# Value products move into a rotation of three PSUM banks with the turns, and the weight mixing is spread differently over a feed-forward block

## The chip, the cores and the metric

The kernel runs on one core of a Trainium2 chip. The metric is the device time of one execution in microseconds (us); for the kernel before it was 3378.83 us, the median of three runs (3373.61 to 3381.02). In the text, PE is the matrix engine (a weight load, PEld, comes before each matmul), DVE the vector engine, ACT the scalar engine, POOL the general engine, and SP the engine whose queue issues all the DMAs of this kernel. Each of them works through its own queue strictly in order and waits on semaphores for the others. Matmuls write into PSUM, which has eight banks of 128 x 512 float32; everything here is float32.

## The reference, cut to what matters

The input x has 4 sequences of 2048 rows of 512 values. The first half is windowed attention, the second a feed-forward layer whose weights differ from sequence to sequence.

```python
x = x + layernorm(attention(layernorm(x), w_qkv))     # 16 heads of 32, windows of 128 rows
x = x + layernorm(ffn(layernorm(x), ...))

# attention: a window of 128 queries sees its own 128 keys and those of both neighbours (384 in all,
# 256 at the ends of a sequence)
scores = einsum('bhnqe,bhnke->bhnqk', q * scale, k_ctx)
out    = einsum('bhnqk,bhnke->bhnqe', softmax(scores), v_ctx)

# feed-forward: a gate makes 8 coefficients g per sequence, which mix 8 expert weights into the base weights
g   = mean_over_rows(relu(x @ gate_w1.T + gate_b1) @ gate_w2.T + gate_b2)
mW1 = W1 + einsum('be,efh->bfh', g, TW1)               # per sequence: 2048 x 512
mW2 = W2 + einsum('be,ehf->bhf', g, TW2)               # per sequence: 512 x 2048
out = gelu(x @ mW1.T + mb1) @ mW2.T + mb2
```

## The kernel before, in words

The order of the instructions on every engine is the order of the Python statements; nothing reorders them.

**Attention** is a loop over 256 slots `i`, four per window (`W_ = i // 4`, 64 windows); a slot handles four heads (`g = i % 4`). Its parts on PE are:

- `scores(i + 1)` (L505): the scores of the next slot, into two double banks of `ps_s`. DVE then takes the row maxima (`nm`, L514) and ACT the exponentials (`pr`, L527, `exponentials`), four per slot.
- `turn(i, j)` (L542): four 128x128 transposes of `pr` for key block `j`, into a bank of the pool `ps_t`; ACT copies them to `prT` (L544). There are three turns in a slot (`nk == 3`), and two where the window stands at an end of a sequence.
- `values(i)` (L559): 12 (or 8) small matmuls with V, into a bank `po` of the pool `ps_o`, which has one bank for a whole window; after the window's fourth slot ACT copies all 512 columns to `oT` (L567).
- `fore[i]` and `dense[i]`: other matmul work laid between. They are pieces of the q, k, v projections (L438, seven products for each of the three, of four 128x256 matmuls each, all through the one bank `pm` of `ps_m`), or of the gate (`pmg`, L163, eight times half of a 128x512 matmul). Each ends with a copy or an addition by ACT or DVE (`produced`) which frees the bank. `dense` is split into two halves, one on either side of the third turn.
- `mid[i]`: in each slot with `i % 4 == 0`, four transposes `pto` (L248) of the finished window's `oT` into a bank of `ps_t`, read by DVE (L255, `out_scaled`). `aux[i]`: transposes `ptx` (L277) or `pt_a` (L364) into `ps_t`, copied out by ACT.

`rest[i]` is DVE, POOL and DMA work (norms, residuals, loads). From slot 84 on, one or two steps of the weight mixing follow (`MIXED`, 21 in 16 slots). The placement repeats every 16 slots; `p = i % 16` is called the position. Gate pieces stand at p = 12 to 15; projection pieces at p = 0 to 11, with a `dense` in each and a `fore` as well unless `p % 4 == 0`. `ptx` stands at p = 0, 4, 8 and 11.

**Mixing** (`mixer`) is a generator that also runs through the feed-forward stage. One step is one DVE instruction `acc = exps * g + acc` (L144) on 128x1024 values, whose expert weights (512 KB) SP loads three steps ahead into four buffers; after eight such steps a ninth makes sums (L152 to L155), and the results go to DRAM. There are 576 steps in all.

**Feed-forward** is a loop over 16 blocks `K` of 512 rows, four to a sequence. The first half of a block has four sets (`begin`, `middle`, `end`), each of seven products of four 128x256 matmuls (L753) and adds on DVE: `cpa` (L799), `cpb` (L808), `cpv` (L811), each reading a bank. The seventh product of a set (`A22`, in `end`) accumulates into the bank that `cpv` reads, and stands behind four products of the next set; for the last set it stands in the second half, after a quarter of product 0. `middle` calls `step()` four times: before `cpa`, before `cpb`, before `cpv` and after it. The second half has seven products (`product2`, L846), each with an add by DVE (L865) that frees its bank. Each asks SP for the weights of three products ahead (`w2s`) as soon as it is done, and then for mixing steps before its add. Product 3 and product 5 share a bank. After product 6, `finish` writes results, and `load_x1` waits until those have left (SP: `fx<-x1d`).

A block takes 33 mixing steps: four in each set, and 3, 3, 2, 3, 3, 2, 1 in the products. The last block of a sequence takes two in each set. `last_end[2]` (matmuls `pb`, L232 and L233) forms a bias vector of the last sequence from the coefficients that `last_end[1]` computes after product 5 of block 0.

Of the kernel before, what the change touches and what calls it, by code (L numbers as in the profile page):

```python
# [9 lines left out]
F32 = mybir.dt.float32  # L10
# [3 lines left out]
PSUM = bass.MemoryType.PSUM  # L14
DRAM = bass.MemoryType.DRAM

P = 128
NB, L, D = 4, 2048, 512
H, E = 16, 32
W = 128  # L20
NW = L // W
KC = D // P
# [12 lines left out]
def sandwich(ctx: ExitStack, tc: tile.TileContext, x, w_qkv, gw1, gb1, gw2, gb2, w1, b1, w2, b2, tw1, tb1, tw2, tb2, out):  # L35
    nc = tc.nc
# [277 lines left out]
    with ExitStack() as actx:  # L314
# [1 line left out]
        work = actx.enter_context(tc.tile_pool(name="work", bufs=2))  # L316
        wp2 = actx.enter_context(tc.tile_pool(name="wp2", bufs=1))
        ps_s = actx.enter_context(tc.tile_pool(name="ps_s", bufs=2, space=PSUM))
        ps_t = actx.enter_context(tc.tile_pool(name="ps_t", bufs=2, space=PSUM))
        ps_o = actx.enter_context(tc.tile_pool(name="ps_o", bufs=1, space=PSUM))  # L320
        ps_m = actx.enter_context(tc.tile_pool(name="ps_m", bufs=1, space=PSUM))

        def load_tile(K, t, tag, bufs):
# [105 lines left out]
        def product(K, i, u, half):  # L429
            l, r, begins, _, _ = products[u]  # L430
            if begins and half == 0:
                bank[0] = ps_m.tile([P, 2, Q], F32, tag="pm", name=f"pm_{K}_{i}_{u}")
            if u < 2 and half == 0:
                rights.setdefault(K, {"11": xnT_of[K][:, :2, :Q], "21": xnT_of[K][:, 2:, :Q]})
            left, right = lefts[i][l], rights[K][r]
            for kc in range(2):
                a, b = (left, right) if i < 2 else (right, left)
                nc.tensor.matmul(  # L438
                    bank[0][:, half, :],
                    lhsT=a[:, kc, ts(half, P)],  # L440
                    rhs=b[:, kc, :],
                    start=(begins and half == kc == 0),
                    stop=True,
                    skip_group_check=True,
                )
# [20 lines left out]
        def span_of(W_):  # L466
            b, w = divmod(W_, NW)
            lo, hi = max(w - 1, 0), min(w + 1, NW - 1)
            return b * NW + lo, hi - lo + 1
# [49 lines left out]
        def exponentials(i, heads):  # L519
            W_, g = divmod(i, KC)  # L520
            nk = span_of(W_)[1]
            st = win[W_]
            scs = st["sc", g]
            for r in heads:
                h = g * 4 + r
                pr = work.tile([P, 3 * W], F32, tag="pr", bufs=8, name=f"pr_{i}_{r}")
                nc.scalar.activation(  # L527
                    pr[:, : nk * W],
                    scs[r // 2][:, r % 2, : nk * W],
                    AF.Exp,  # L530
                    bias=st["nm"][:, h : h + 1],
                    accum_out=st["den"][:, h : h + 1],
                )
                st["pr"][h] = pr

        def turn(i, j):

            W_, g = divmod(i, KC)
            st = win[W_]
            pt = ps_t.tile([P, 4, W], F32, tag="pt", name=f"ptp_{i}_{j}")  # L540
            for r in range(4):
                nc.tensor.transpose(pt[:, r, :], st["pr"][g * 4 + r][:, ts(j, W)], ident)  # L542
            prT = work.tile([P, 4, W], F32, tag="prT", bufs=4, name=f"prT_{i}_{j}")
            nc.scalar.copy(prT, pt)  # L544
            st["prT"][g, j] = prT

        def values(i):

            W_, g = divmod(i, KC)
            lo, nk = span_of(W_)  # L550
            st = win[W_]
            if g == 0:
                st["po"] = ps_o.tile([P, KC, P], F32, tag="po", name=f"po_{W_}")
            for j in range(nk):
                kb, jj = divmod(lo + j, WB)
                prT = st["prT"].pop((g, j))
                for r in range(4):
                    h = g * 4 + r
                    nc.tensor.matmul(  # L559
                        st["po"][r * E : (r + 1) * E, g, :],  # L560
                        lhsT=v_of[kb][:, jj, h * E : (h + 1) * E],
                        rhs=prT[:, r, :],
                        start=(j == 0),
                        stop=(j == nk - 1),
                    )
            if g == KC - 1:
                nc.scalar.copy(st["oT"], st.pop("po"))  # L567


        slots = range(-16, NS + 64)  # L570
        fore = {i: None for i in slots}
        dense = {i: None for i in slots}
# [3 lines left out]
        mid = {i: [] for i in slots}  # L576
        late = {i: [] for i in slots}
        for K in range(1, NBK):
            s0 = 4 * (4 * K - 5)
            if K > 1:  # L580
                for t in range(WB):

                    i = s0 - 14 + 4 * t if K > 2 else s0 + t - 3
# [6 lines left out]
            for i in range(3):  # L590
                for u in range(7):

                    (fore if u % 2 else dense)[s0 + 4 + 4 * i + (u + 1) // 2] = (
                        lambda half, K=K, i=i, u=u: product(K, i, u, half),
# [13 lines left out]
        def gate_tile(K, oc, half):  # L608
            if half == 0:
                bank[0] = ps_m.tile([P, TB], F32, tag="pm", name=f"pmg_{K}_{oc}")  # L610
            gate_matmuls(bank[0], gT_of[K], oc, range(2 * half, 2 * half + 2))

        gate_at = {K: 4 * (4 * (K + 3) - 5) for K in range(11)} | {11: 204, 12: 220, 13: 236, 14: 248}
        for K, s0 in gate_at.items():
            first[s0 - 2].append(lambda K=K: load_gate(K))
            for oc in range(KC):
                dense[s0 + oc] = (
                    lambda half, K=K, oc=oc: gate_tile(K, oc, half),
# [30 lines left out]
        for W_ in range(NWA - 1):  # L649
# [4 lines left out]
            i = 4 * W_ + 8 if W_ < 58 and W_ % WB != 1 else 4 * W_ + 7  # L654
# [36 lines left out]
        for i in range(NS):  # L691
            W_, g = divmod(i, KC)
            nk = span_of(W_)[1]
            for f in first[i]:
                f()
            if i + 1 < NS:
                scores(i + 1)
            more = i + 1 < NS
            if fore[i]:
                fore[i][0](0)  # L700
                fore[i][0](1)
                if more:
                    exponentials(i + 1, (0, 1))
                fore[i][1]()

            for f in rest[i]:
                f()
            if i >= 84:
                for _ in range(MIXED[i % 16]):
                    next(blend)  # L710
            turn(i, 0)
            turn(i, 1)
            if dense[i]:
                dense[i][0](0)
            if more:
                exponentials(i + 1, (2,) if fore[i] else (0, 1))
            for f in mid[i]:
                f()
            if nk == 3:
                turn(i, 2)  # L720
            if more:
                exponentials(i + 1, (3,) if fore[i] else (2, 3))
            if dense[i]:
                dense[i][0](1)
                dense[i][1]()
            for f in aux[i][:1]:
                f()
            values(i)
            for f in aux[i][1:] + late[i]:
                f()  # L730


    with ExitStack() as fctx:
# [186 lines left out]
        def finish(K, t, y, sm):  # L920
            b, k = divmod(K, NBLK)
            x1 = x1s.pop((K, t))
            normalize(y, y, sm)
            nc.vector.tensor_tensor(x1, x1, y, ALU.add)
            nc.sync.dma_start(out[b, k * TB + t * P : k * TB + (t + 1) * P], x1)
# [28 lines left out]
        def gate_last(n):  # L954
# [5 lines left out]
        last_end = gate_end(NB - 1, hsum_of[NB - 1], spare, spare_bank)  # L960
# [6 lines left out]
            ("product", 0, 2): [lambda: gate_last(0), lambda: gate_last(1)],  # L967
            ("product", 0, 4): [last_end[0]],
            ("product", 0, 5): [last_end[1]],
            ("product", 0, 6): [last_end[2]],  # L970
        }

        for c in range(0, HC, 2):
# [8 lines left out]
        def mixing(*counts):  # L982

            counts = iter(counts)

            def steps():
                for _ in range(next(counts)):
                    next(blend, None)

            return steps  # L990

        for K in range(NBK):
            b, k = divmod(K, NBLK)
            if k == 0:
                mb2_of[b] = io.tile([P, D], F32, tag="mb2", bufs=1, name=f"mb2_{b}")
                nc.sync.dma_start(mb2_of[b], mb2_d[b])
            before = None
            for c in range(0, HC, 2):
                n = K * (HC // 2) + c // 2
                S = begin(n)  # L1000

                if n < 2:
                    step = mixing(0, 0, 0, 0)
                elif K == 0 or (k == NBLK - 1 and b + 1 < NB):
                    step = mixing(0, 1, 0, 1)
                else:
                    step = mixing(1, 1, 1, 1)
                middle(n, S, before, step)
                before = (n, S)
                if pending:  # L1010
                    finish(*pending.pop(0))
                for f in hooks.get(("set", n), ()):
                    f()
            for j, _ in enumerate(second(K, before, mixing(3, 3, 2, 3, 3, 2, 1), load_x1)):

                if j == (0 if K else 3) and K + 1 < NBK:
                    load_block(K + 1)
                if j == (2 if K else 5) and K + 1 < NBK:
                    right_sums(K + 1)
                for f in hooks.get(("product", K, j), ()):  # L1020
                    f()
# [58 lines left out]
```

## Time and profile before

| | |
|---|---|
| median of three runs | 3378.83 us |
| profiled execution, its own time | 3378.4 us |
| its span | 3376.6 us |
| PE busy | 3298.4 us (98%) |
| DVE busy | 2142.4 us (63%) |
| ACT busy | 1524.6 us (45%) |
| granted PE clock, mean | 0.996 |

The span is what the trace covers; times inside the trace are counted from its start. The attention loop runs until 1780 us, the feed-forward stage from there to the end. A busy time is the union of an engine's instructions; matmuls overlap in the records, so the distance from one start to the next is a better measure of what a group of matmuls takes than its busy time. An arrow behind an instruction names what ended the idle time of its engine before it.

### The profile page before, as it was taken

To read this page: it belongs to the slowest core of one execution; us is meant where nothing else is said; L and a number is where in the kernel's file an instruction comes from. 1 tells how busy PE (TensorE), PEld (TensorE's weight loads), DVE (VectorE), ACT (ScalarE), POOL (GpSimd) and SP (SyncE) were. 2 spreads that over 40 slices of the span, in tenths; PEclk is the share of its full clock that TensorE was granted. 3 is DMA by queue.
4 is the path that set the end of the run, shared out by engine and by line. 5 is a ranking of instruction groups with operands and counts; after the bars stand their busy time and mean duration, and the time that the engine had idled before them with its cause. 6 is when DMAs were issued, how large, how long until landed. Compare 5 with 4: busy or idle time off the path is not lost.

```text
span 3376.6 us, 58332 instructions
## 1 busy us (share of the span) xinstructions
PE 3298.4 (98%) x22824; PEld 2611.7 (77%) x22824; DVE 2142.4 (63%) x3008; ACT 1524.6 (45%) x3957; POOL 652.9 (19%) x776
## 2 busy tenths in 40 slices
PE   8999999999999999999999999999999999999998
PEld 4777777777677777767658888888888888888887
DVE  3655555787888788877774676567766766622222
ACT  2767767677666776667773211122221112222111
POOL 0101010111111111111112122233222222312222
PEclk9999999999999999999999999999999999999999
DMA  2111111454554555544567788988899888832332
GB/s 83 45 54 45 54 51 51 153 166 164 184 172 158 164 181 184 170 157 162 181 225 262 273 323 316 354 295 311 305 349 353 319 311 297 315 107 103 125 122 78
DMA packets 316118, 651.95 MB, mean 193 GB/s; under 512 B 22969, under 2 KB 89657, under 8 KB 295490
## 3 DMA queue, kind: packets, MB, share of 16 engines
q1 hardware_dynamic: 315842, 648.22, 55.0%
q8 instruction: 179, 2.93, 0.4%
q14 instruction: 97, 0.79, 0.1%
HBM read 538.03 MB, written 110.10 MB: 192 GB/s over the span
## 4 chain that ended last, share of the span: by engine, by line
PE 87%; DVE 6%; DMA 5%; ACT 1%; issue 1%; SPq 0%; DVEq 0%; ACTq 0%
PE pm L438 16%; PE px L753 13%; PE ptp L542 8%; PE px L846 8%; PE sc L505 7%; PE pz L753 7%; PE pmg L163 6%; PE po L559 6%; DMA exps<-in_tw 4%; PE pz L846 4%; PE py L753 3%; PE py2b L846 3%; PE py L846 2%; DVE acc L144 2%; PE pm L378 1%; DVE nm L514 1%
## 5 line engine op out<-in xcount | busy, mean ns | idle before, releaser
L144 DVE SCALAR_TENSOR_TENSOR acc<-exps,g,acc 128x1024 f32<-128x1024 f32 x512 | 686.1, 1340 | 244.6 <-DMA exps<-in_tw 239.4
L527 ACT ACTIVATE pr<-sc,nm 128x384 f32<-128x384 f32 (+1 forms) x1024 | 580.0, 575 | 254.3 <-DVE nm L514 254.3
L514 DVE TENSOR_REDUCE nm<-sc 128x2 f32<-128x768 f32 (+1 forms) x512 | 449.5, 919 | 358.4 <-PE sc L505 357.9
L544 ACT COPY prT<-ptp 128x512 f32<-128x512 f32 x736 | 406.8, 589 | 224.3 <-PE ptp L542 216.9
L786 ACT COPY cpa<-px 128x512 f32<-128x512 f32 x64 | 37.5, 586 | 868.2 <-PE px L753 868.1
L542 PE MATMUL ptp<-ident,pr 128*128 128x128 f32 x2944 | 407.3, 275 | 2.6 <-ACT prT L544 2.6
L542 PEld LDWEIGHTS ptp<-ident,pr 128*128 128x128 f32 x2944 | 339.7, 141 | 90.5 <-issue 54.9
L753 PE MATMUL px<-tT,w 128*128 128x256 f32 x1536 | 355.1, 379 | 0.6 <-DVE cpv L811 0.6
L753 PEld LDWEIGHTS px<-tT,w 128*128 128x128 f32 x1536 | 291.8, 190 | 40.6 <-DVE cpv L811 1.0
L846 PE MATMUL px<-w2s,u 128*128 128x256 f32 x1024 | 233.0, 384 | 17.2 <-DVE y L865 16.5
L505 PE MATMUL sc<-k,q 32*128 32x384 f32 (+2 forms) x2816 | 246.9, 422 | 2.9 <-ACT pr L527 2.9
L846 PEld LDWEIGHTS px<-w2s,u 128*128 128x128 f32 x1024 | 196.1, 192 | 47.6 <-DVE y L865 19.8
L163 PE MATMUL pmg<-gT,gw_sb 128*128 128x512 f32 x480 | 224.4, 593 | 0.0
L559 PE MATMUL po<-prT,v 128*32 128x128 f32 x5888 | 216.3, 277 | 6.5 <-ACT prT L544 6.4
L527 ACT ACTIVATION_READ_ACCUMULATOR pr<-sc,nm 128x1 f32 x1024 | 212.7, 208 | 0.0
L559 PEld LDWEIGHTS po<-prT,v 128*32 128x32 f32 x5888 | 144.4, 109 | 76.4 <-issue 63.1
L92 POOL TENSOR_SCALAR ve_b<-mv_b 128x1 f32<-128x1 f32 x64 | 14.2, 222 | 952.4 <-DVE mv_b L90 907.3
L438 PE MATMUL pm<-xnT,wqkv 128*128 128x256 f32 x720 | 181.2, 388 | 0.0
L823 POOL TENSOR_TENSOR t<-u 128x512 f32<-128x512 f32 x64 | 86.4, 1351 | 489.1 <-ACT u L765 484.8
L505 PEld LDWEIGHTS sc<-k,q 32*128 32x128 f32 x2816 | 120.5, 183 | 59.2 <-issue 44.7
L438 PEld LDWEIGHTS pm<-xnT,wqkv 128*128 128x128 f32 x720 | 127.2, 190 | 38.7 <-issue 21.9
L808 DVE TENSOR_TENSOR cpb<-pz,cpb 128x512 f32<-128x512 f32 x64 | 44.1, 689 | 148.6 <-PE pz L753 145.1
(164 smaller groups left out, 5291.8 us busy)
## 6 DMA issues: line engine op xcount, KB each, us to landing
exps<-in_tw SPq DMA_DIRECT2D x512, 512.0 KB, 5.8
w2s<-m2d SPq DMA_DIRECT2D x112, 1024.0 KB, 7.6
acc<-in_w SPq DMA_DIRECT2D x64, 512.0 KB, 6.6
x<-in_x SPq DMA_DIRECT2D x64, 256.0 KB, 3.5
m1d<-acc SPq DMA_DIRECT2D x64, 256.0 KB, 6.5
m2d<-acc SPq DMA_DIRECT2D x64, 256.0 KB, 6.1
w<-m1d SPq DMA_DIRECT2D x16, 1024.0 KB, 8.9
fxT<-xTd SPq DMA_DIRECT2D x16, 1024.0 KB, 9.9
```

The lines of the kernel that those rows point to most:

```text
L144: nc.vector.scalar_tensor_tensor(acc, ets.pop(n), g_all[b][:, e : e + 1], acc, ALU.mult, ALU.add)
L163: nc.tensor.matmul(pm, lhsT=gw1_sb[:, kc, ts(oc, P)], rhs=xT[:, kc, :], start=(kc == 0), stop=(kc == KC - 1))
L438: nc.tensor.matmul(bank[0][:, half, :], lhsT=a[:, kc, ts(half, P)], rhs=b[:, kc, :], start=(begins and half == kc == 0), stop=True, skip_g ...
L505: nc.tensor.matmul(scs[r // 2][:, r % 2, col : col + nj * W], lhsT=q[rows, g, ts(W_ % WB, W)], rhs=k_of[kb][rows, g, j0 * W : (j0 + nj) * ...
L514: nc.vector.tensor_reduce(st["nm"][:, h : h + 2], scs[u][:, :, : nk * W], AX.X, ALU.max, negate=True)
L527: nc.scalar.activation(pr[:, : nk * W], scs[r // 2][:, r % 2, : nk * W], AF.Exp, bias=st["nm"][:, h : h + 1], accum_out=st["den"][:, h : h ...
L542: nc.tensor.transpose(pt[:, r, :], st["pr"][g * 4 + r][:, ts(j, W)], ident)
L544: nc.scalar.copy(prT, pt)
L559: nc.tensor.matmul(st["po"][r * E : (r + 1) * E, g, :], lhsT=v_of[kb][:, jj, h * E : (h + 1) * E], rhs=prT[:, r, :], start=(j == 0), stop= ...
L753: nc.tensor.matmul(bank[:, f, :], lhsT=factor[:, f, kc * P : (kc + 1) * P], rhs=right[:, kc, :], start=(start and f == 0 and kc == 0), sto ...
L823: nc.gpsimd.tensor_tensor(t1s[c], b12, S["u"][:, :, :Q], ALU.subtract)
L846: nc.tensor.matmul(bank[:, t, :], lhsT=right(c - c % 2)[:, c % 2, ts(t, P)], rhs=w[:, c, :], start=(start and c == t == 0), stop=True, ski ...
```

## The change

Three things are changed.

1. The pool `ps_o` is dropped and `ps_t` gets a third bank. `values(i)` takes a bank of that rotation for its slot, and ACT copies the slot's 128 columns to `oT` right after it: 256 copies of 128x128 in place of 64 of 128x512.
2. Within a slot, the three turns now stand together, then the remaining exponentials, then `mid`, then `rest` and the mixing steps, and then both halves of `dense` without anything between them.
3. In feed-forward blocks that take four steps in each set, a set now takes 1, 2, 1, 2 steps; the products of every block take 2, 2, 1, 2, 2, 2, 1. That is 36 steps in such a block instead of 33, and 20 instead of 25 in the last block of a sequence. The bias matmuls `last_end[2]` move from after product 6 of block 0 to after product 0 of block 1.

```diff
-        ps_t = actx.enter_context(tc.tile_pool(name="ps_t", bufs=2, space=PSUM))
-        ps_o = actx.enter_context(tc.tile_pool(name="ps_o", bufs=1, space=PSUM))
+        ps_t = actx.enter_context(tc.tile_pool(name="ps_t", bufs=3, space=PSUM))
...
-            if g == 0:
-                st["po"] = ps_o.tile([P, KC, P], F32, tag="po", name=f"po_{W_}")
+            po = ps_t.tile([P, KC, P], F32, tag="pt", name=f"po_{i}")
...
-                        st["po"][r * E : (r + 1) * E, g, :],
+                        po[r * E : (r + 1) * E, 0, :],
...
-            if g == KC - 1:
-                nc.scalar.copy(st["oT"], st.pop("po"))
+            nc.scalar.copy(st["oT"][:, g, :], po[:, 0, :])
...
+            for j in range(nk):
+                turn(i, j)
+            if more:
+                exponentials(i + 1, (2, 3) if fore[i] else range(4))
+            for f in mid[i]:
+                f()
 
             for f in rest[i]:
                 f()
             if i >= 84:
                 for _ in range(MIXED[i % 16]):
                     next(blend)
-            turn(i, 0)
-            turn(i, 1)
             if dense[i]:
                 dense[i][0](0)
-            if more:
-                exponentials(i + 1, (2,) if fore[i] else (0, 1))
-            for f in mid[i]:
-                f()
-            if nk == 3:
-                turn(i, 2)
-            if more:
-                exponentials(i + 1, (3,) if fore[i] else (2, 3))
-            if dense[i]:
                 dense[i][0](1)
                 dense[i][1]()
...
-            ("product", 0, 6): [last_end[2]],
+            ("product", 1, 0): [last_end[2]],
...
-                    step = mixing(1, 1, 1, 1)
+                    step = mixing(1, 2, 1, 2)
...
-            for j, _ in enumerate(second(K, before, mixing(3, 3, 2, 3, 3, 2, 1), load_x1)):
+            for j, _ in enumerate(second(K, before, mixing(2, 2, 1, 2, 2, 2, 1), load_x1)):
```

## The prediction

> **What bounds the kernel now.** First the page: the busy times, and the chain that ended last.
>
> ```profile
> span 3376.6 us, 58332 instructions
> PE 3298.4 (98%) x22824; PEld 2611.7 (77%) x22824; DVE 2142.4 (63%) x3008; ACT 1524.6 (45%) x3957; POOL 652.9 (19%) x776
> PE 87%; DVE 6%; DMA 5%; ACT 1%; issue 1%; SPq 0%; DVEq 0%; ACTq 0%
> ```
>
> PE carries the chain, so a change can win only where PE waits, or runs a group slower than the same group elsewhere. Second, the busy times by stretch (length, then PE, PEld, DVE, ACT, POOL, clock, DMA share, GB/s): a stretch of attention, and the two halves of block 3.
>
> ```profile
> 800.00:1200.00 400.00, 393.31 (x3592) 284.93 (x3592) 322.06 (x473) 277.01 (x747) 59.53 (x88) 1.00 0.52 171
> 2088.20:2136.60 48.40, 48.40 (x226) 42.59 (x226) 28.43 (x44) 18.96 (x42) 12.22 (x15) 1.00 0.87 325
> 2136.60:2189.90 53.30, 50.13 (x226) 43.57 (x225) 30.14 (x36) 0.98 (x3) 13.40 (x9) 0.97 0.99 364
> ```
>
> In attention DVE (81%) and ACT (69%) have room and the DMAs are half idle. In block 3 the DMAs are full (0.99) in the second half, which takes 53.3 us instead of 48.4. Third, PE's instructions in order of time, where I compare distances between starts. A slot at position 9 (start, duration):
>
> ```profile
> 515.62 1.04 PE L542 MATMUL ptp<-ident,pr 128*128 128x128 f32 x8
> 516.64 1.13 PE L438 MATMUL pm<-tx,wsum 128*128 128x256 f32 x4
> 517.60 0.60 PE L542 MATMUL ptp<-ident,pr 128*128 128x128 f32 x4
> 518.04 1.03 PE L438 MATMUL pm<-tx,wsum 128*128 128x256 f32 x4
> 519.00 0.86 PE L559 MATMUL po<-prT,v 128*32 128x128 f32 x24
> ```
>
> Four transposes take 0.44 us (517.60 to 518.04), so eight should take 0.87; here 1.02 pass. The dense piece waits 0.15 for bank `pm`, which DVE's addition for the fore piece frees (515.89 plus 0.69 = 516.58). Waiting, its first matmul also loses the overlap of its weight load: the half takes 0.96 instead of 0.87. A slot at position 8, PE and then DVE:
>
> ```profile
> 760.72 1.03 PE L438 MATMUL pm<-wqkv,xnT 128*128 128x256 f32 x4
> 762.18 0.66 PE L277 MATMUL ptx<-ident,x 128*128 128x128 f32 x4 [0.43 <-DVE x L255]
> ...
> 759.89 1.28 DVE L144 SCALAR_TENSOR_TENSOR acc<-exps,g,acc 128x1024 f32<-128x1024 f32 x1
> 761.44 0.69 DVE L255 TENSOR_TENSOR x<-pto,rden 128x512 f32<-128x512 f32 x1
> ```
>
> `ptx` starts 1.46 us after the dense half instead of 0.87: with two banks it takes the one of `pto`, which DVE reads only after a mixing step. Block 0's end, and block 3's product 5:
>
> ```profile
> 1884.39 2.04 PE L232 MATMUL pb<-tb_sb,gcb 8*128 8x512 f32 x2 [3.87 <-DVE mb L226]
> 1888.07 3.78 PE L753 MATMUL px<-fxT,w 128*128 128x256 f32 x8
> 2174.44 8.69 PE L846 MATMUL px<-w2s,u 128*128 128x256 f32 x32 [3.17 <-DVE y L865]
> ```
>
> Both times DVE stands behind mixing steps whose weights have not landed. Last, SP and DVE after the start of block 5 at 2288.5:
>
> ```profile
> 2299.03 1.00 SPq L918 DMA_DIRECT2D fx<-x1d  x2
> 2300.36 0.38 SPq L119 DMA_DIRECT2D exps<-in_tw  x1
> ...
> 2305.26 1.28 DVE L144 SCALAR_TENSOR_TENSOR acc<-exps,g,acc 128x1024 f32<-128x1024 f32 x1 [4.94 <-DMA exps<-in_tw]
> ```
>
> SP stands 10.5 us before `load_x1`, with all expert loads behind it; the fourth step of the block starts at +16.8. Three loads are ahead by then, and `cpv` of set 0 needs three steps.
>
> **Attention, part by part.** In brackets: slots. Projections stand in slots 0 to 235, 15 rounds of 16; four rounds begin at a sequence's end with two turns at p = 0 to 3, which gain nothing.
>
> (a) Fore and dense with an ACT copy, p = 1, 2, 5, 6, 9, 10 (11 x 2 + 15 x 4 = 82). Before, from the first turn to the values 519.00 - 515.62 = 3.38. After: 12 transposes at 0.109, eight matmuls at 0.216 and 0.09 of change to the narrow tile = 3.13. DVE's addition ends 0.96 after the first turn starts, the turns 1.31. Gain 0.25 x 82 = 20.5.
>
> (b) p = 3, 7, 11 (11 + 15 + 15 = 41): the slot takes 6.79, or 7.26 with `ptx`; the same sum gives 6.61 and 7.08. Gain 0.18 x 41 = 7.4.
>
> (c) p = 0, 4, 8: with three banks `ptx` takes the one of the second turn, whose copy is done long before. At p = 4, 8 from slot 84 on (20) a slot goes from 6.37 to 5.71, the length that it has before mixing starts; at p = 0 (11) from 6.53 to 5.74. Against that `pto` follows the turns directly and takes the first turn's bank: its copy ends 1.33 after the turn's start, the turns end after 1.37, and a late weight load adds some 0.08. Gain 0.58 x 20 + 0.71 x 11 = 19.4.
>
> (d) That 0.08 is a loss at p = 4, 8 before slot 84 (10) and at p = 12 (14): -1.9.
>
> (e) Slots without filling, 240 to 247, and four gate slots after them lose a wait of the third turn: 0.1 to 0.2 each, +2.
>
> Sum 47.4 us. **New operation:** a 128x128 copy on ACT. The trace has none. Between 0.21 (the 128x1 read of L527) and 0.59 (128x512); L527's two sizes, 588 and 485 ns, give 0.8 ns a column, so 0.28, nearer the lower. Four for one adds 0.53 us per window to ACT. It is hidden: in a fore slot ACT is done 0.5 us into the next slot, and the third turn, which takes the bank in the worst order, comes 3.5 us in (1.8 without fore). Were ACT late by more than that, PE would wait by the excess. The exponentials now follow three copies instead of two; they still end 0.7 us before the scores need the bank, as today. On DVE, `out_scaled` passes `rest` and mixing, which is why (c) holds; the mixing steps and SP's loads for them move later in a slot, past nothing that SP issues in between. DVE waits for the scores 1.5 us at a time on average (waits: 357.9 us in 236), 0.1 at the least; a slot shorter by 0.25 leaves it on time or 0.15 late, which the 0.7 covers.
>
> **Feed-forward.** (f) `pb` moves: block 0's product 6 plus wait takes 11.04 (1873.35 to 1884.39) instead of 6.91; the two pairs 3.68 at half clock instead of 1.8 (in attention); block 1's first two products 6.58 instead of 3.45. Gain 4.1 + 1.9 + 3.1 = 9.1. At its new place its inputs are ready for 60 us.
>
> (g) Waits in second halves, as excess over 6.91 per product: blocks 1 to 10 lose 2.7, 0.7, 5.0, 1.9, 0, 0.7, 2.4, 2.1, 5.3, 1.3 = 22.1. Before product 5 can start, 11 steps must be done, after it will be seven. Each product's loads queue behind 1 MB of `w2s`: today 3 x 0.5 + 1 MB per 6.9 us, with the rest 364 GB/s and full; then 2 x 0.5 + 1. I take 20 off.
>
> (h) First halves of blocks 1, 2, 4, 5, 6, 8, 9, 10 carry 24 steps instead of 16. `cpv` of set 0 now needs the fourth step, and A22 behind it stands at +17.3 (ten products of 1.73). Today that step starts at +16.8, so `cpv` would end at 18.7: 1.4 late. In the last set `cpv` needs 22 steps by 48.4. DVE: 24 steps at 1.3 to 1.34 with sums some 34 us, adds 7.2, `finish` and its statistics 7, less the last two steps: 45.6, plus the wait for the loads, up to 5: up to 2 late. A stall delays PE as a whole, so the larger counts. From 0 (the loads come sooner after a lighter second half) to 5 (the whole load wait stays): I take 1.5, because today's block recovers from a lag of 7 us. Loss 1.5 x 8 = 12.
>
> Today's stall of 3.17 us before product 5 is followed by 3.4 us at half clock in the same trace (product 5 takes 8.52, not 6.91); one of 2.54 is not. So the price of a stall rises by 1.6 from about 3 us on; (g) holds it for blocks 3 and 9. The Trainium skill (TensorE: Matmul & The Clock Gate, What's actually happening) puts the drop after an idle window of about 3.4 us; by it those two stalls would not have slowed PE, and (g) would be 3.4 us smaller. The row decides.
>
> Sum 47.4 + 9.1 + 20 - 12 = 64.5. From the profiled execution's 3378.4 that is 3313.9; the median of the runs is 0.4 above it, so **3314 us**.
>
> **Rivals.**
>
> *The first halves fall behind and it gets slower* (7%). If loads there land as slowly as in today's second halves (9.4 us from issue, by median, against 5.6), four buffers give a step per (9.4 + 1.3) / 4 = 2.7 us. From +17, 15.5 more steps end at 59, and `cpv` comes 11 late; with 2 for the half clock 13 x 8 = 105. Then 3378 - 76.5 + 105 = 3407. It decides from 9.6 us per block. For it: DVE is at 94% there by (h), and 36 steps a block against 33. Against it: without `w2s` the first halves move 290 to 325 GB/s today and landing is at 5.6.
>
> *The stalls only move* (20%): 5 us in each of the eight first halves, 3314 + 28 = 3342. For it: SP's 10.5 us before `load_x1` is not touched.
>
> *The turns don't cover the addition* (8%): if DVE comes 0.4 us later than today, dense waits still, and (a) and (b) go: 3342. Against it: the row maxima start at the same time in nearly every slot.
>
> **How the numbers follow.** Forecast 60%, rivals 35%, the rest unforeseen. Low end: no stall in first halves, all of (g), 2 more from slots after a gate: 3314 - 12 - 2 - 2 = 3298, taken to 3295. High end: stalls of 5 and half of (a) and (b) missing: 3342 + 14 = 3356, cut to 3350. 0.2% is 7 us, about what a measurement can tell from no change (the runs spread over 7.4). Faster: 0.6 + 0.2 + 0.08 and part of the rest, 0.90; slower 0.08.
>
> **What would show it.** Right: twelve transposes 1.31 us apart from dense with no wait, slots at p = 9 of 6.6 and at p = 8 of 5.8 us; attention ends near 1733; no wait before `pb`; product 5 on time. Wrong: idle PE before `po` or `pto` by ACT; PE behind `cpv` (L811) early in set 1 or in product 0, then a half clock; block lengths above 99 us.

## The result, and the profile after

The changed kernel takes 3385.15 us (median of 16 runs, 3375.15 to 3387.85); the kernel before took 3378.27 us beside it (16 runs, 3372.96 to 3381.72). The ratio is 1.0019 [1.0011, 1.0026]: it is 0.2% slower, where 1.9% faster was forecast. The profiled execution has a span of 3379.8 us against 3376.6. Its page, as far as it answers to the lines shown of before:

```profile
span 3379.8 us, 58589 instructions
PE 3286.9 (97%) x22824; PEld 2633.6 (78%) x22824; DVE 2159.3 (64%) x3008; ACT 1530.1 (45%) x4149; POOL 698.8 (21%) x776
PE 84%; DMA 7%; DVE 5%; issue 2%; ACT 2%; SPq 0%; DVEq 0%; ACTq 0%
```

PE's share of the chain fell from 87% to 84%, and the DMAs' rose from 5% to 7%. A total that hardly moves hides two large movements. The balance of the two traces (the length of a block is the distance from its first product to that of the next):

| part | before, us | after, us | difference |
|---|---|---|---|
| start of the feed-forward stage | 1773.6 | 1729.6 | -44.0 |
| block 0 | 114.5 | 106.8 | -7.7 |
| blocks 3 and 7 (20 steps now) | 200.7 | 193.4 | -7.3 |
| blocks 1, 2, 4, 5, 6, 8, 9, 10 (36 steps now) | 792.0 | 854.4 | +62.3 |
| blocks 11 to 15 | 495.8 | 495.7 | -0.1 |

The sum is -59.0 - 0.1 + 62.3 = +3.2, the difference of the spans. A block in which PE never waits takes 96.69 us (blocks 12 to 14 in both traces), and block 1 now holds the 2.1 us of `pb`. So the eight blocks lose 854.4 - 8 x 96.69 - 2.1 = 78.8 us, 9.8 each. Before, attention ended at 1773.6, not at the 1780 from which the prediction's 1733 was counted; its 47.4 us would put the end at 1726, and it came at 1729.6. Of the 44.0 us, 2.2 lie ahead of the first scores (60.3 instead of 62.5 us), a time that spreads from 59.8 to 63.9 over all the profiles; 41.8 lie in the loop.

**Attention did nearly as forecast.** PE's instructions after the change, in a slot at position 9 and in one at position 8 (start, duration):

```profile
518.38 1.47 PE L541 MATMUL ptp<-ident,pr 128*128 128x128 f32 x12
519.69 1.89 PE L437 MATMUL pm<-xnT,wsum 128*128 128x256 f32 x8
521.51 0.86 PE L557 MATMUL po<-prT,v 128*32 128x128 f32 x24
...
740.52 0.66 PE L248 MATMUL pto<-ident,oT 128*128 128x128 f32 x4
741.01 1.89 PE L437 MATMUL pm<-wqkv,xnT 128*128 128x256 f32 x8
742.74 0.60 PE L277 MATMUL ptx<-ident,x 128*128 128x128 f32 x4
743.27 0.86 PE L557 MATMUL po<-prT,v 128*32 128x128 f32 x24
```

From the first turn to the values 3.13 us pass (before 3.38), the twelve turns take 1.31, and the eight dense matmuls are no longer broken by a wait. `ptx` follows its dense piece after 1.73 for eight matmuls, which is the pure matmul time; before, 1.46 passed for the last four alone.

**The first halves did not.** PE's waits over the whole feed-forward stage, after:

```profile
PE px L745 <- DVE cpv L803: 52.1, 24, 5.6
PE py L745 <- DVE cpa L791: 1.0, 1, 1.0
PE px L838 <- ACT last L282: 0.7, 1, 0.7
```

and the longest before:

```profile
PE px L846 <- DVE y L865: 16.5, 8, 3.4
```

The waits before product 5 (16.5 us in eight, before) are gone; 24 waits on `cpv` by products of the first halves stand in their place, eight of them (33 us) by the last A22, in product 0. The waits on `cpv` and `cpa` and the half clock behind them account for the whole loss: 53.1 us of waits, and nine stretches of 51.2 us in all at a granted clock of 0.50, which cost half of that, 25.6; together 78.7.

Where DVE's time went is seen in block 6. Busy times by stretch (length, PE, PEld, DVE, ACT, POOL, clock, DMA share, GB/s), first half before, then both halves after, then both halves of block 3 after:

```profile
2385.20:2433.60 48.40, 48.40 (x226) 42.59 (x226) 38.89 (x50) 18.83 (x42) 15.50 (x15) 1.00 0.85 305
```

```profile
2360.70:2419.80 59.10, 52.84 (x236) 45.04 (x236) 49.37 (x56) 20.07 (x44) 16.12 (x12) 0.98 0.92 319
2419.80:2466.40 46.60, 46.60 (x214) 40.93 (x214) 27.14 (x33) 0.01 (x1) 13.46 (x12) 0.99 0.85 306
2048.20:2096.60 48.40, 48.40 (x226) 42.63 (x225) 24.40 (x33) 18.91 (x42) 10.44 (x11) 1.00 0.81 284
2096.60:2144.90 48.30, 48.30 (x226) 42.53 (x225) 28.25 (x33) 0.92 (x3) 14.78 (x13) 1.00 0.93 334
```

The second half of block 3 takes 48.3 instead of 53.3. The first half of block 6 takes 59.1 instead of 48.4, and DVE, busy for 38.9 of 48.4 before, is busy for 49.4. SP and then DVE from the start of block 6 at 2360.7, after:

```profile
2361.36 0.39 SPq L119 DMA_DIRECT2D exps<-in_tw  x1
2362.84 1.54 SPq L917 DMA_DIRECT2D out<-fx  x2
2370.45 0.94 SPq L910 DMA_DIRECT2D fx<-x1d  x2
2371.45 0.94 SPq L119 DMA_DIRECT2D exps<-in_tw  x2
...
2369.91 1.28 DVE L144 SCALAR_TENSOR_TENSOR acc<-exps,g,acc 128x1024 f32<-128x1024 f32 x1 [1.33 <-DMA exps<-in_tw]
2371.11 0.68 DVE L800 TENSOR_TENSOR cpb<-pz,cpb 128x512 f32<-128x512 f32 x1
2376.23 1.28 DVE L144 SCALAR_TENSOR_TENSOR acc<-exps,g,acc 128x1024 f32<-128x1024 f32 x1 [4.44 <-DMA exps<-in_tw]
2377.43 0.68 DVE L803 TENSOR_TENSOR cpv<-px,cpv 128x512 f32<-128x512 f32 x1
```

What SP waited for there (2360 to 2373), in us, times and longest:

```profile
SPq L910 <- DMA out<-fx: 6.2, 2, 6.0
```

SP stands for 6.0 us until `load_x1` at +9.8, since the place that it loads into is free only when the `out` stores have left. Behind it stand the expert loads. The fourth step of the block starts at +15.5, 4.4 us late, and `cpv` of set 0 ends at +17.4, just about when A22 needs it (+17.3). That one wait costs PE nothing here. But DVE carries the lag through the rest of the half. PE at the end of the first half:

```profile
2411.77 0.60 PE L838 MATMUL px<-w2s,u 128*128 128x256 f32 x2
2416.31 2.62 PE L745 MATMUL px<-tT,w 128*128 128x256 f32 x8 [3.94 <-DVE cpv L803]
2418.72 6.45 PE L838 MATMUL px<-w2s,u 128*128 128x256 f32 x24
```

The matmuls after that wait take 0.30 us each instead of 0.22; the clock in the stretch behind it:

```profile
2417.50:2420.90 3.40, 3.40 (x10) 2.69 (x9) 3.30 (x6) 0.84 (x2) 1.69 (x1) 0.50 0.76 292
```

`cpv` of the sets ends at +17.4, +30.5, +44.4 and +55.5; where DVE keeps up with PE, as in six of these blocks before, the last ends at +47.6, and PE needs it by about +48.4. What DVE itself waited for in that half, before (2385.20 to 2432.30) and after (2360.70 to 2415.60), with the us in total, the times and the longest:

```profile
DVE acc L144 <- DMA exps<-in_tw: 6.8, 2, 5.0
DVE cpb L808 <- PE pz L753: 2.3, 1, 2.3
```

```profile
DVE acc L144 <- DMA exps<-in_tw: 8.2, 4, 4.4
DVE y L857 <- PE py2b L838: 2.7, 1, 2.7
```

Before, DVE had caught up with PE again and waited for it (`cpb`); after, it never does within the half: its wait for `py2b` lies at the very start, for product 6 of the block before. In the first halves of the eight blocks, up to the last `cpv`, it waits 5.8 to 11.1 us for loads (8.5 on average), and from the first load wait on for PE not once.

### The profile page after: what moved, and what is told of

Its sections match the earlier page's. It is cut to its first block, busy times and chain, and to the rows that moved or that the text cites. A ratio compares the mean times of both kernels' runs of the same rounds, so it can differ in the third digit from the quotient of the medians.

```text
span 3379.8 us, 58589 instructions
## 1 busy us (share of the span) xinstructions
PE 3286.9 (97%) x22824; PEld 2633.6 (78%) x22824; DVE 2159.3 (64%) x3008; ACT 1530.1 (45%) x4149; POOL 698.8 (21%) x776
## 4 chain that ended last, share of the span: by engine, by line
PE 84%; DMA 7%; DVE 5%; issue 2%; ACT 2%; SPq 0%; DVEq 0%; ACTq 0%
PE pm L437 17%; PE ptp L541 10%; PE px L838 9%; PE px L745 8%; PE pz L838 7%; PE sc L504 6%; PE pmg L163 6%; PE po L557 5%; DMA exps<-in_tw 5%; PE pz L745 4%; PE py L838 3%; PE py2b L838 2%; DVE acc L144 2%; PE py L745 2%; DMA out<-fx 1%
## 5 line engine op out<-in xcount | busy, mean ns | idle before, releaser
L144 DVE SCALAR_TENSOR_TENSOR acc<-exps,g,acc 128x1024 f32<-128x1024 f32 x512 | 697.6, 1362 | 174.8 <-DMA exps<-in_tw 169.5
L543 ACT COPY prT<-ptp 128x512 f32<-128x512 f32 x736 | 385.9, 593 | 170.1 <-PE ptp L541 165.6
L745 PE MATMUL px<-tT,w 128*128 128x256 f32 x1536 | 374.2, 391 | 52.1 <-DVE cpv L803 52.1
L745 PEld LDWEIGHTS px<-tT,w 128*128 128x128 f32 x1536 | 297.9, 195 | 103.6 <-DVE cpv L803 62.5
L541 PE MATMUL ptp<-ident,pr 128*128 128x128 f32 x2944 | 375.0, 277 | 0.0
L541 PEld LDWEIGHTS ptp<-ident,pr 128*128 128x128 f32 x2944 | 332.3, 142 | 54.3 <-issue 36.3
L92 POOL TENSOR_SCALAR ve_b<-mv_b 128x1 f32<-128x1 f32 x64 | 47.7, 746 | 877.1 <-DVE mv_b L90 877.1
L526 ACT ACTIVATION_READ_ACCUMULATOR pr<-sc,nm 128x1 f32 x1024 | 224.3, 219 | 0.0
L163 PE MATMUL pmg<-gT,gw_sb 128*128 128x512 f32 x480 | 215.9, 593 | 0.0
L163 PEld LDWEIGHTS pmg<-gT,gw_sb 128*128 128x128 f32 x480 | 86.5, 190 | 86.1 <-issue 86.1
```

Of the source, the lines that this page charges most:

```text
L144: nc.vector.scalar_tensor_tensor(acc, ets.pop(n), g_all[b][:, e : e + 1], acc, ALU.mult, ALU.add)
L163: nc.tensor.matmul(pm, lhsT=gw1_sb[:, kc, ts(oc, P)], rhs=xT[:, kc, :], start=(kc == 0), stop=(kc == KC - 1))
L526: nc.scalar.activation(pr[:, : nk * W], scs[r // 2][:, r % 2, : nk * W], AF.Exp, bias=st["nm"][:, h : h + 1], accum_out=st["den"][:, h : h ...
L745: nc.tensor.matmul(bank[:, f, :], lhsT=factor[:, f, kc * P : (kc + 1) * P], rhs=right[:, kc, :], start=(start and f == 0 and kc == 0), sto ...
```

## The experiments

Times stand beside the kernel before on the same chip.

**The two halves of the change apart.** e1 keeps the new attention and the place of `pb`, with the old mixing; e2 is the kernel before with the new mixing and the new place of `pb`.

```diff
# e1, against the kernel after
-                    step = mixing(1, 2, 1, 2)
+                    step = mixing(1, 1, 1, 1)
...
-            for j, _ in enumerate(second(K, before, mixing(2, 2, 1, 2, 2, 2, 1), load_x1)):
+            for j, _ in enumerate(second(K, before, mixing(3, 3, 2, 3, 3, 2, 1), load_x1)):
# e2, against the kernel before
-            ("product", 0, 6): [last_end[2]],
+            ("product", 1, 0): [last_end[2]],
...
-                    step = mixing(1, 1, 1, 1)
+                    step = mixing(1, 2, 1, 2)
...
-            for j, _ in enumerate(second(K, before, mixing(3, 3, 2, 3, 3, 2, 1), load_x1)):
+            for j, _ in enumerate(second(K, before, mixing(2, 2, 1, 2, 2, 2, 1), load_x1)):
```

> The attention part of the change with the place of the bias matmuls, and the mixing steps of before (1, 1, 1, 1 in a set; 3, 3, 2, 3, 3, 2, 1 in the products). Theory: the whole loss of the changed kernel lies in the first halves of the eight blocks with 36 steps, and the rest is independent of it. Then the attention stage ends 44 us earlier, as in the changed kernel, block 0 is 8 us shorter, the waits before product 5 are back (some 22 us with their half clock), and the time is 3378 - 52 = 3326. Rival: the feed-forward stage loses to the shorter attention (the mixing is no further, but the loads meet it in another state): over 3345.

> The mixing part and the place of the bias matmuls alone, with the attention of before. Theory: the feed-forward stage takes 1650 us as in the changed kernel (1603 before), so 3378 + 47 = 3425, with PE waiting for the cpv add in the same eight blocks. If the two parts disturb each other, it is under 3400.

e1 took 3322.63 us, 0.9836 [0.9820, 0.9853]: attention ends at 1730.7, and PE again waits 11.3 us in eight places before product 5. e2 took 3429.55 us, 1.0151 [1.0130, 1.0171], with the 36-step blocks at 105.4 to 109.5 us and 56.8 us of waits on `cpv`. Against the kernel before that is -1.64% and +1.51%; with the 8.8 us of `pb` counted once instead of twice, the two add up to +0.13%, and the whole change measured +0.19%. The loss belongs to the mixing, and attention has no visible part in it.

**Which limit in the first half?** Three theories: A, SP's stand before `load_x1` delays the loads, and a DVE without slack cannot make up for it; or the work of DVE is by itself too long; or the DMAs cannot bring 24 steps in time. e3 issues `load_x1` after the first set of the next block, with `finish` for those rows a set later. e4 takes the expert loads away: from load 211 on the steps read a tile that already lies there, so the mixed weights of the later sequences are not those of the reference.

```diff
# e3, against the kernel after
-                load_x1(K, t)
+                if K == NBK - 1:
+                    load_x1(K, t)
...
-                if pending:
+                if K and c == 0:
+                    for t in range(2):
+                        load_x1(K - 1, t)
+                elif pending:
# e4, against the kernel after (kept holds the last tile loaded)
+            if n > 210:
+                ets[n] = kept[0]
+                return
...
```

> The changed kernel, with the two loads of x1 that end a block issued after the first set of the next block, and the two finish steps that use them one set later; so SP no longer stands before them, for the results of the block before to leave, with the expert loads of the first set behind it. Theory A (the steps start late because their loads stand behind x1, and DVE has no room to catch up): the expert waits of a first half go from 8 to 10 us to under 3, the blocks from 106 to 97 to 99 us, the time to 3305 to 3325. Theory B (24 steps and the adds fill DVE whatever the loads do): blocks stay above 103 us, the time above 3360. Theory C (the DMAs cannot deliver 24 steps in a first half): the waits only move to the later sets, the time stays above 3360 as well.

> The changed kernel without the expert loads of the feed-forward stage: from step 211 of the expert loads on, the steps read one tile that is already there, so the mixed weights of the later sequences are not the right ones; base weights are still loaded and results stored. DVE does all its work. Theories A and C (loads): PE waits for no cpv, the blocks take 97 us, the time is 3385 - 80 = 3305 (3300 to 3312). Theory B (DVE is full): PE still waits over 4 us in each of the eight blocks, the time is above 3340.

e3 took 3332.70 us, 0.9864 [0.9841, 0.9887]; e4 3308.92 us, 0.9794 [0.9774, 0.9813]. Of e3, DVE's wait for loads in the first half of block 6 and PE's waits on `cpv` in the whole feed-forward stage:

```profile
DVE acc L144 <- DMA exps<-in_tw: 1.9, 3, 0.9
...
PE px L745 <- DVE cpv L803: 19.0, 8, 4.4
```

The stretch of that half in e3 (columns as above):

```profile
2330.70:2379.10 48.40, 48.40 (x225) 42.34 (x223) 45.75 (x53) 18.09 (x40) 13.21 (x11) 1.00 1.02 366
```

The same half in e4, and then PE's waits on `cpv` in e4 (its lines stand five further down):

```profile
2323.60:2372.00 48.40, 48.40 (x226) 42.61 (x225) 44.95 (x54) 18.35 (x41) 13.17 (x11) 1.00 0.39 131
```

```profile
PE px L750 <- DVE cpv L808: 2.3, 3, 1.2
```

Against a waitless 775.6 us (8 x 96.69 + 2.1) the eight blocks lose 78.8 us after the change, 26.2 in e3 (801.8) and 3.1 in e4 (778.7). So with these 24 steps the place of `load_x1` (and of the `finish` that moves with it) is worth 52.6 us, the loads in the better order 23.1, and DVE's own work 3.1. The two runs of e3 lie 10.6 us apart, and its profile is of the faster one; by the medians the place is worth 52.4. That is short of theory A, which had e3 at 3305 to 3325. DVE's work does fit: 45.0 busy in 48.4. It leaves 3.4 us, less than the load waits of each of the eight halves after the change (5.8 to 11.1). In e3 the DMAs are full in that half (share 1.02, 366 GB/s; block 3's full second half before had 364), which may explain the remaining 23 us; no run separates that from the order of the other loads.

**The stalls moved within the half.** e5 moves one step in every set from before `cpv` to behind it.

```diff
-                    step = mixing(1, 2, 1, 2)
+                    step = mixing(1, 2, 0, 3)
```

> The changed kernel with steps 1, 2, 0, 3 in a set instead of 1, 2, 1, 2: as many steps, but one fewer ahead of every cpv add. Theory A (PE waits for cpv because it stands in DVE's queue behind the steps): the stall of the last set, 3.9 to 5.6 us, shrinks by one step of 1.3 to 2 us and its half clock partly with it; the waits of set 1 at +18 to +22 go, since cpv of set 0 needs only the prefetched three again; blocks of 103 to 104 instead of 106, the time 3360 to 3370. If the DMAs alone set the pace (theory C) and cpv is late by the whole lag in any place, less than 8 us are gained.

3373.12 us, 0.9991 [0.9981, 1.0001]: some 9 us better than the change by the two ratios, between what theories A and C gave. PE's waits within the sets fall from 20 to 7 us in all, but those in product 0 stay (35 us, before 33; each is now 4.1 to 4.7). So in both placements most of the lag reaches the last `cpv`. An early stall delays PE too and gives DVE that time to catch up; without it the lag is still there at the end.

**Order and banks apart.** e6 has the new order in a slot with the old banks, e7 the new banks with the old order; both have the old mixing and the old place of `pb`.

```diff
# e6, against the kernel before, in a slot: the turns together, then mid, rest and mixing, dense undivided
+            for j in range(nk):
+                turn(i, j)
+            if more:
+                exponentials(i + 1, (2, 3) if fore[i] else range(4))
...
-            turn(i, 0)
-            turn(i, 1)
...
# e7, against the kernel before
-        ps_t = actx.enter_context(tc.tile_pool(name="ps_t", bufs=2, space=PSUM))
-        ps_o = actx.enter_context(tc.tile_pool(name="ps_o", bufs=1, space=PSUM))
+        ps_t = actx.enter_context(tc.tile_pool(name="ps_t", bufs=3, space=PSUM))
...
+            nc.scalar.copy(st["oT"][:, g, :], po[:, 0, :])
```

> The kernel before with the new order of a slot alone, old banks (two for the turns, one for the values of a window), old mixing. Theory: the order needs the third bank. The third turn takes the bank of the first, whose copy ends 1.33 us after the first turn's start, when two turns have taken 0.87: 0.45 us more in a gate slot (56), 0.26 more in a slot with a fore piece (123), 0.1 less at p = 0, 4 and 8: 25 + 32 - 3, so 3378 + 54 = 3432. Rival: most of the gain comes from the order (dense pieces undivided, the addition covered) and the bank is a detail: under 3378.

> The kernel before with the new banks alone (values in the rotation of three, copied by slot), old order and old mixing. Theory: only ptx gains, at p = 0, 4 and 8 (31 slots by 0.6 on average); dense still waits for the addition: 3378 - 18 = 3360. The 128x128 copy on ACT takes 0.28 us. Rival (the bank gives most of the attention gain): under 3345.

e6 took 3444.21 us, 1.0197 [1.0176, 1.0217]; e7 3362.67 us, 0.9954 [0.9939, 0.9970]. PE's waits in attention on the copy of a turn, in e6, and then the same in the kernel before:

```profile
PE ptp L542 <- ACT prT L544: 66.0, 221, 1.5
```

```profile
PE ptp L542 <- ACT prT L544: 2.6, 9, 0.3
```

With two banks the third turn stands right behind the second and waits for the copy of the first, 0.3 us in nearly every slot, and the slots lengthen: slots at position 9 go from 6.86 to 7.13, gate slots from 7.01 to 7.53. With three banks in the old order only positions 0, 4 and 8 gain (6.53 to 5.94, and 6.37 to 5.78). Counted from the first scores on, the order alone costs 71 us of attention, the banks alone gain 13, and both together gain 42: terms (a) and (b) need the third bank and the order at once. e6 came out 12 us above its 3432, e7 within 3 of its 3360.

**16, 20 or 24 steps in the first half, with `load_x1` early or late.** e8 is e1 with the late load. e9 and e10 take 1, 1, 1, 2 in a set and 2 in each product (34 steps in a block), e9 with the late load, e10 with the early one; both take the third turn behind two exponentials again in slots that have neither `fore` nor `dense`, to see whether the half clock goes that showed there after the change (slots 242, 243, 246 and 247). e11 is like e9 with 1, 1, 0, 3 and without that change of the slots.

```diff
# e9 and e10, against the kernel after (e11: mixing(1, 1, 0, 3))
-                    step = mixing(1, 2, 1, 2)
+                    step = mixing(1, 1, 1, 2)
...
-            for j, _ in enumerate(second(K, before, mixing(2, 2, 1, 2, 2, 2, 1), load_x1)):
+            for j, _ in enumerate(second(K, before, mixing(2, 2, 2, 2, 2, 2, 2), load_x1)):
# e9 and e10, slots without filling
-            for j in range(nk):
+            filled = fore[i] or dense[i]
+            for j in range(nk if filled else 2):
                 turn(i, j)
+            if not filled:
+                if more:
+                    exponentials(i + 1, (0, 1))
+                if nk == 3:
+                    turn(i, 2)
...
# e8, e9 and e11 also have the late load_x1 of e3
```

> The attention part and the place of the bias matmuls (as in e1), with the mixing of before, and x1 loaded after the first set. Theory: the waits before product 5 come from the loads of the second half itself (11 steps ahead of the add), so they stay, 14 us in all: 3318 to 3323. Rival: they come from the lag that the first set starts with, then 3305 to 3310.

> The changed kernel with 1, 1, 1, 2 steps in a set and 2 in each product (20 + 14 = 34 a block), x1 loaded after the first set, and in the slots without dense or fore piece the third turn again behind the first two exponentials. Theory A: 20 steps leave DVE room to catch up, 8 steps ahead of the add that frees product 5's bank leave no wait there: blocks of 97 to 97.5, feed-forward 25 us shorter than in e1; and without the bunched turns the half clock in slots 240 to 247 goes, 4 to 5 us: 3323 - 20 - 5 = 3298. If blocks are bound by the sum of the loads of a block (34 steps, 33 in e1), they stay at 98 to 99: over 3312.

> As e9, but x1 loaded at the end of the block as in the changed kernel. Theory A: SP stands 8 to 10 us before x1 again and the first set's fourth step comes at +16, but three steps are enough for cpv of set 0, and DVE has more room than with 24: a lag of 5 us at +17 shrinks to 1 to 3 by the last set; PE waits 0 to 2 there, so 3298 to 3312. If x1 alone were the cause (whatever the number of steps), it loses as much as the changed kernel against e3, some 50 us: 3345.

> As e9, but with 1, 1, 0, 3 steps in a set (one fewer ahead of cpv) and with the slot order of the changed kernel in all slots. Theory A: no wait for cpv in either, so the feed-forward stage is as long as in e9 within 3 us; the half clock in slots 240 to 247 is back: 4 to 5 us more than e9.

| steps in a first half | `load_x1` early | `load_x1` late |
|---|---|---|
| 16 | e1: 3322.63 us, 0.9836 [0.9820, 0.9853] | e8: 3324.30 us, 0.9841 [0.9825, 0.9858] |
| 20 | e10: 3320.73 us, 0.9822 [0.9806, 0.9838] | e9: 3303.31 us, 0.9772 [0.9756, 0.9788] |
| 24 | the change: 3385.15 us, 1.0019 [1.0011, 1.0026] | e3: 3332.70 us, 0.9864 [0.9841, 0.9887] |

e11 took 3304.84 us, 0.9778 [0.9760, 0.9796]. PE's waits in e9 from 1705 us, in the last slots of attention, to the end:

```profile
PE sc L504 <- ACT pr L526: 1.4, 4, 0.5
PE px L844 <- ACT last L282: 0.7, 1, 0.7
PE po L557 <- ACT prT L543: 0.3, 1, 0.3
```

No wait on DVE is listed: blocks 2 to 14 take 96.69 us, but for 97.03 in block 9, and block 1 98.80. This is the best version, faster than both kernels, though 5 us above theory A's 3298. PE's waits on `cpv` in e10, over the same time:

```profile
PE px L751 <- DVE cpv L809: 11.7, 9, 2.7
```

The late load is worth nothing at 16 steps (where the loss lies before product 5: 11.3 us of waits in e1, 10.7 in e8), 17 us at 20 and 52 at 24. So the price of the same stand of SP grows with the steps. DVE's free time falls with them, but the loads grow in number too, and the second half has 17, 14 and 12 steps, so the table alone does not say which of these it is. Read down a column, the steps are worth more than the load: from 24 to 20 steps the time falls by 64 us with the early load and by 29 with the late one. Either remedy alone removes most of the 78.8 us (26.2 are left in e3, 15.8 in e10), so the loss needs both, SP's stand and the 24 steps. e10 came out 9 us above what was expected of it.

## Why the prediction was wrong

- **(a) to (d)** held nearly to the hundredth: p = 9 takes 6.61 (6.6 forecast), p = 8 5.79 (5.8), p = 0 5.82 (5.74 and the 0.08 of the late weight load), p = 3 6.61, p = 11 7.08, and p = 12 loses 0.07. The ACT copy of 128x128 has a median of 0.265 us (0.28 estimated).
- **(e)** failed with a small sum: slots 242, 243, 246 and 247 take 6.5 to 6.8 us instead of 5.47, under a half clock, -4.8 us for +2. Attention gave 44.0 of 47.4, of which 2.2 came ahead of the first scores and belong to no term.
- **(f)** held: 7.7 in block 0 and 3.2 in block 1 that now starts at full clock, less 2.1 for `pb` there: 8.8 of 9.1.
- **(g)** held: no wait before product 5 is left, so all 22.1 went, of which 20 were counted.
- **(h) is the step that failed**: "From 0 (the loads come sooner after a lighter second half) to 5 (the whole load wait stays): I take 1.5, because today's block recovers from a lag of 7 us." The mechanism, `cpv` late and PE behind it, was right, and DVE's work was about right (45.6 said, 45.0 busy in e4's block 6). The size was wrong: 78.8 us instead of 12. In the kernel before DVE has slack in such a half: it waits 2 to 12 us for PE there, and so recovers. The eight steps that the change adds, some 10.5 us, use that up. The recovery was carried over to a half from which the same edit takes what made it possible. And the upper end was not an upper end: 5 is one load wait (4.94), while the waits for loads in a first half add up to 8.5 us on average (5.8 to 11.1). With 8.5, the prediction's own sum for the last set, 45.6 + 8.5 - 48.4, gives 5.7 us late; PE waited 6.6 us a block. Half clock behind the stalls adds 3.2 us a block, which the term did not hold.
- SP's "10.5 us before `load_x1`" was read as one stand. Within them SP still issued a load of `w2s`, an expert load and two stores; the stand itself, after the second store, was 5.9 us (2293.18 to 2299.03).

The rival of first halves that fall behind came about with 9.8 us per block, just past the 9.6 from which it was to decide, and the sign follows. Its condition did not: loads land there in 5.9 us by median (5.4 before), not in 9.4. What it named as speaking for it, a DVE at 94%, was the ground; the delay came mostly from SP's queue (52.6 of the 78.8 us, by e3). The rival that had SP's stand for it had the right cause, with half the price. The two belonged together, at more than the first one's 7%. The sign that it named is in part luck, as its price of 13 us a block rested on loads that land late, and they did not.

A gain of 64.5 us was forecast, and between the two profiles a loss of 3.2 came (6.9 by the medians). Of the difference of 67.7, (h) is 66.8, attention 3.4 and (f) 0.3, and (g) takes 2.1 off; this closes to 0.7.

## What to carry to other kernels

Before work is moved to a stretch, list the idle time of the engine that gets it and what today absorbs lateness there: the moved work takes that reserve, and a lag that "recovers today" then reaches the bound engine in full, with the clock's price on top. An upper end for such a term goes by the sum of all the waits in the stretch, not by the longest. Where one queue issues all loads in order, a load that must wait for a store belongs behind the loads that are needed first; moving it was worth 52 us with 24 steps (e3), 17 with 20 (e9) and nothing with 16 (e8). Moving less work was worth more still: four steps fewer in a half gained 64 us with the old place of that load. The best time came from both.

## What the runs showed of the clock

Two things were not expected. First, PE's clock halved in attention's last slots although no wait there exceeds 0.71 us. The stretch before such a drop, after the change, and the drop itself, and then PE's instructions there (start, duration, idle before):

```profile
1642.70:1646.11 3.41, 2.45 (x33) 1.24 (x25) 2.01 (x4) 2.63 (x10) 0.78 (x2) 1.00 0.90 297
1646.11:1649.52 3.41, 3.41 (x30) 2.99 (x28) 2.61 (x3) 1.69 (x4) 0.00 (x0) 0.50 1.02 348
```

```profile
1644.10 0.93 PE L504 MATMUL sc<-k,q 32*128 32x128 f32 x8 [0.70 <-ACT pr L526]
1645.23 0.93 PE L504 MATMUL sc<-k,q 32*128 32x128 f32 x8 [0.19 <-ACT pr L526]
1646.09 2.82 PE L541 MATMUL ptp<-ident,pr 128*128 128x128 f32 x12
```

PE is busy for 72% of the stretch before the drop. Less did not always cause a drop: in the kernel before, in the same slots, this stretch was followed by full clock (it begins 57 times 3.413 us before the drop at 1884.0; what that means is said below):

```profile
1689.44:1692.85 3.41, 2.29 (x30) 1.62 (x28) 3.16 (x6) 2.70 (x8) 0.06 (x1) 1.00 1.00 414
```

PE is busy for 67% of it. And e7, in the old order, has a drop (behind waits of 0.9 and 1.2 us), and e9, which restores the old place of the third turn there, still has three drops. The bunching of the turns is therefore not the cause that it was taken for, and what sets these drops stays open.

Second, the length of a stall does not decide. In e3 one of 1.93 us in product 0 of block 1 was followed by a drop, one of 3.04 in block 10 was not:

```profile
1884.91 3.47 PE L745 MATMUL px<-tT,w 128*128 128x256 f32 x8 [1.93 <-DVE cpv L803]
...
2781.24 1.99 PE L745 MATMUL px<-tT,w 128*128 128x256 f32 x8 [3.04 <-DVE cpv L803]
```

The same eight matmuls take 3.47 and 1.99 us. So the prediction's "about 3 us" is no threshold. The place of the stall tells them apart: in each of the 13 profiles all drops begin whole multiples of 3.413 us apart, and every drop ahead of the last block lasts a multiple of 3.41 us. On this grid the shorter stall of e3 lies within one window, while the longer one is shared by two:

```profile
1881.89:1885.30 3.41, 1.48 (x8) 0.98 (x7) 3.41 (x5) 1.26 (x3) 1.22 (x1) 0.99 0.99 346
2776.18:2779.59 3.41, 2.02 (x10) 1.44 (x8) 3.34 (x6) 0.91 (x2) 0.71 (x2) 1.00 1.04 373
2779.59:2783.01 3.42, 1.77 (x8) 1.59 (x9) 3.38 (x4) 0.91 (x2) 1.40 (x2) 1.00 0.98 340
```

PE is busy for 1.48 us in the one, and for 2.02 and 1.77 in the others. In blocks 1 to 14 of all the profiles this border holds: the windows before the 36 drops have PE busy for at most 0.44 of the window, and of the other windows at full clock none has less than 0.41. The drops in attention's last slots lie above it, so there busy time alone is not the measure. The Trainium skill (TensorE: Matmul & The Clock Gate, What's actually happening) has a free-running window of 3413 ns, which agrees with this grid. That the drop needs an idle window does not agree: PE was busy in 1.48 of the 3.41 us before the drop at 1885.3 in e3.
